# Layer 1 attention: each batch's second 128 queries taken in reversed blocks of 32, and one product of 512 columns for both halves

## The chip, the core and the metric

The kernel runs on one core of a Trainium2 chip. The metric is the time on the device in microseconds (us), as the median of several runs; less is better. The engines named below work side by side, each through its own instructions in order: PE (matrix products), DVE (vector work), ACT (scalar functions and copies), POOL (general work and gathers by index), SP (starts most transfers).

## The reference

Two transformer layers on x of 8 batches x 256 tokens x 128 channels. Each layer adds attention and a mixture of experts, both computed from the same normalised input. The change is in layer 1's attention:

```python
q = (x @ Wq + bq).reshape(B, T, 8, 128);  kv = x @ Wkv + bkv      # 8 query heads, one key and value head
q = q + pe;  k = k + pe                                           # the same table of positions
scores = einsum('bhqd,bkd->bhqk', q, k) / sqrt(128)
scores = where(tril(ones(T, T)), scores, lowest)                  # causal
out = softmax(scores) @ v                                         # then heads side by side
return out @ Wo
```

with T = 256 here. Layer 0's attention has 16 heads of 8 channels and no mask. Both layers' experts pick tokens by a router; layer 0 takes two experts of eight per token and a shared one, layer 1 takes one of eight.

## The kernel before

All of it is float32, and every matrix product runs as two passes over PE. The order of the work is written out by hand: a call wrapped in `seq` keeps its place in the program on its engine, and tables (`at_place`, `at1`, read by `between` and `fill`) name the steps that are put between the attention's own. Layer 0 goes through its 8 batches with the routing, the experts, the shared expert (`shared_up`, `shared_down`) and, at the end, the first three blocks of layer 1's norm between them. Layer 1 goes through its 8 batches with its own router and experts between them.

**Norm and projections.** `Norm.turned` transposes a block of 512 normalised tokens with PE into a tile of the PSUM pool `one` (tag `bank`, three buffers taken in turn; a fourth, `held`, is for one long-lived tile) and ACT copies it into `xT`, channels on partitions, 2048 tokens in order. `l1_values` makes values and router logits from it (line 784), `l1_project` queries for 8 heads and keys (line 807), to which DVE adds bias and positions (line 814). `l1_scale` multiplies the query weights, biases and positions (`peq_s`) by 1/sqrt(128) on POOL, once. POOL also builds the constants at the start (`more_constants`); the norm's reciprocal roots (lines 303 and 304) are POOL instructions behind them.

**Layer 1's attention.** A batch has three parts: `u[0]` is the first 128 queries of all 8 heads against 128 keys, `u[1]` and `u[2]` are the second 128 queries of 4 heads each against 256 keys. For each part:
- `l1_scores` (line 1281): PE, into a tile of 1024 columns of the PSUM pool `big`, which has two such tiles;
- `l1_maxima` (lines 1291 and 1295): DVE adds the causal mask to the 128 columns on the diagonal and takes the maximum;
- `l1_exp` (line 1301): ACT, one exponential and sum per head;
- `l1_weigh` (line 1313): the division by the sum, on POOL, or on DVE for the parts in `ON_VECTOR`;
- `l1_turn` (line 1328): DVE transposes 32x32 blocks into `pT`, one tile for each half, so that keys lie on partitions: the 32 queries of block n lie in rows 32n to 32n+31.

`l1_pv(b, t, po)` (line 1345) then multiplies with the values. Block n of the queries uses strip n of PE, rows 32n to 32n+31, and its own PSUM bank `po[n]`; the four strips work side by side. The values lie in `vrep`, a copy for each strip, written by `l1_spread`. Block n of half t needs key blocks 0 to 4t+n. Each product has 8 heads x 32 queries = 256 columns:

```python
for j in range(NQ1 * (t + 1)):
    for n in range(NQ1):
        end = NQ1 * t + n
        if j <= end:
            r = ROW * n
            ...
            rhs=pT[r : r + ROW, :, j, :],
```

`l1_out` (line 1358) copies the four banks into `oT` with ACT, and `l1_finish` (line 1364) multiplies by Wo and lets DVE add to `acc`. The products of batch b-1 stand in batch b (`l1_previous`), between the scores of `u[1]` and those of `u[2]`:

```python
l1_exp(u[0])
l1_previous(b)
...
l1_weigh(u[0])
l1_scores(u[2])
```

For the last batch they stand at the end of the program, the halves apart. Buffers in the pool `work` have two copies by default; `oT`, the second half's `pT`, layer 0's attention result and the shared expert's hidden values share tag `c`, the first half's `pT` and layer 0's queries `qa` share tag `h`.

## Time and profile before

| | us |
|---|---|
| median of 3 runs | 591.26 (590.09 to 594.53) |
| the profiled execution | 584.82 |
| its span, first to last instruction | 583.0 |
| busy in it: PE, its weight loads, DVE, ACT, POOL | 497.3, 354.1, 359.4, 246.6, 205.6 |
| line 1345, the products with the values | PE busy for 48.9, 576 records, two per product |
| mean granted TensorE clock | 0.938 |

The profile is of one execution. A line in a view reads: start and length, engine, source line, operation, the tiles it writes and reads (out<-in), shapes and count; in brackets, how long the engine stood idle before it and what ended the wait. A timeline line merges neighbours of one kind. "PEld" is PE's weight loads. In a table of waits the columns are the total, how often, and the longest, in us. The granted clock is 1.0 or 0.5, and a mean over a stretch lies between them. Layer 0 ends near 336 us; layer 1's eight batches begin their scores near 334, 358, 379, 412, 458, 497, 527 and 541 us.

### The profile page before, as it was taken

What the parts mean: (1) busy time and instruction counts of PE and PEld (TensorE: products, weight loads), DVE (VectorE), ACT (ScalarE), POOL (GpSimd) and SP (SyncE); (2) the same over time, 40 slices, a digit from 0 to 9 for tenths busy, and PEclk for the clock granted to TensorE, in tenths of its full rate; (3) what the DMA queues carried; (4) which work ended last, traced back from release to release, by engine and by line L of the source; (5) the groups of instructions that cost most, each with busy time, mean ns of one, the idle gap of its engine ahead of it and who ended that gap; (6) DMA issues with size and microseconds to landing.
All of it is one profiled execution on the core that took longest, in us unless ns stands there. A gap on an engine that the chain in (4) does not pass through costs nothing.

```text
span 583.0 us, 11267 instructions
## 1 busy us (share of the span) xinstructions
PE 497.3 (85%) x3996; PEld 354.1 (61%) x3996; DVE 359.4 (62%) x733; ACT 246.6 (42%) x681; POOL 205.6 (35%) x254
## 2 busy tenths in 40 slices
PE   4887688889998899967899968877969989989777
PEld 1633345656766577543554736666667878978666
DVE  5487954646756467637797467787633544527662
ACT  4616123434443254313443551523255584665161
POOL 6230023266432440274372032212576041124740
PEclk9999786989999799989999997996989999999977
DMA  3600411324443231011021130171048465512111
GB/s 108 189 1 19 133 33 44 110 72 121 126 128 105 74 77 38 28 46 29 17 69 45 37 92 19 37 200 41 25 108 234 145 149 180 158 55 64 33 32 56
DMA packets 61925, 47.78 MB, mean 82 GB/s; under 512 B 6389, under 2 KB 56781, under 8 KB 61869
## 3 DMA queue, kind: packets, MB, share of 16 engines
q1 hardware_dynamic: 57453, 38.59, 23.3%
q0 software_dynamic: 3840, 8.26, 5.9%
q8 instruction: 32, 0.52, 0.4%
q10 hardware_dynamic: 576, 0.20, 0.1%
q14 instruction: 24, 0.20, 0.1%
HBM read 38.78 MB, written 8.26 MB: 81 GB/s over the span
## 4 chain that ended last, share of the span: by engine, by line
PE 56%; DVE 20%; issue 9%; ACT 6%; POOL 4%; DMA 1%; SPq 0%; another core or an unknown queue 0%; POOLq 0%; ACTq 0%; DVEq 0%
PE s L894 7%; PE u L692 6%; PE pv L967 5%; PE s L1281 4%; PE d L709 4%; DVE mx L909 4%; PE u L1210 3%; PE o L1345 3%; PE d L1228 3%; PE qk L807 3%; PE s L940 3%; PE wo L1364 3%; ACT p L1301 2%; PE ds L760 2%; PE sh L745 2%
## 5 line engine op out<-in xcount | busy, mean ns | idle before, releaser
L952 ACT ACTIVATE eT<-s 128x1024 f32<-128x1024 f32 x64 | 65.5, 1024 | 138.9 <-PE s L940 95.7
L909 DVE TENSOR_REDUCE mx<-s 128x4 f32<-128x1024 f32 x64 | 77.7, 1220 | 32.0 <-PE s L940 14.3
L513 POOL DMA_INDIRECT xs<-xd,idx x62 | 63.0, 1016 | 67.0 <-issue 57.8
L894 PE MATMUL s<-qk 32*128 32x256 f32 x512 | 74.4, 422 | 13.6 <-DVE mx L909 8.8
L1313 POOL TENSOR_TENSOR p<-p,rec 128x1024 f32<-128x1024 f32 x21 | 39.8, 1896 | 112.3 <-DVE rec L1311 112.2
L1301 ACT ACTIVATE p<-s,m 128x256 f32<-128x256 f32 (+1 forms) x128 | 52.5, 443 | 62.5 <-DVE m L1295 51.0
L940 PE MATMUL s<-qa,qk 32*128 32x256 f32 x512 | 75.6, 414 | 2.5 <-DVE qa L921 2.3
L894 PEld LDWEIGHTS s<-qk 32*128 32x128 f32 x512 | 43.2, 195 | 41.7 <-DVE mx L909 17.9
L513 POOL DMA_INDIRECT yt<-yg,idx x48 | 48.9, 1020 | 47.1 <-issue 37.2
L1281 PE MATMUL s<-kT,qT 128*128 128x128 f32 (+1 forms) x256 | 49.8, 348 | 9.1 <-ACT p L1301 4.3
L940 PEld LDWEIGHTS s<-qa,qk 32*128 32x128 f32 x512 | 45.9, 192 | 10.6 <-DVE qa L921 5.0
L1345 PE MATMUL o<-pT,vrep 32*128 32x256 f32 x576 | 48.9, 407 | 3.9 <-DVE pT L1328 2.2
L1281 PEld LDWEIGHTS s<-kT,qT 128*128 128x128 f32 x256 | 40.0, 200 | 18.2 <-issue 6.9
L1345 PEld LDWEIGHTS o<-pT,vrep 32*128 32x128 f32 x576 | 40.5, 197 | 11.6 <-DVE pT L1328 2.4
L692 PE MATMUL u<-xg,gu_s 128*88 128x128 f32 x312 | 42.6, 278 | 1.6 <-issue 1.6
L967 PE MATMUL pv<-eT,va 128*32 128x256 f32 x512 | 39.3, 412 | 1.5 <-issue 1.4
L692 PEld LDWEIGHTS u<-xg,gu_s 128*88 128x88 f32 x312 | 37.1, 160 | 3.8 <-issue 3.8
L1219 ACT ACTIVATE h<-u,own_b 128x128 f32<-128x128 f32 x92 | 25.9, 375 | 27.7 <-PE u L1210 25.2
L1291 DVE TENSOR_TENSOR s<-s,mask 128x512 f32<-128x512 f32 (+1 forms) x24 | 20.9, 869 | 25.2 <-PE s L1281 21.5
L1364 PE MATMUL wo<-wo_s,oT 128*128 128x128 f32 x256 | 34.0, 297 | 2.1 <-DVE qT L814 1.8
L1364 PEld LDWEIGHTS wo<-wo_s,oT 128*128 128x128 f32 x256 | 33.0, 212 | 3.9 <-issue 3.3
L1328 DVE STREAM_TRANSPOSE pT<-p 128x1024 f32<-128x1024 f32 x24 | 29.5, 1232 | 7.1 <-POOL p L1313 7.1
(222 smaller groups left out, 843.2 us busy)
## 6 DMA issues: line engine op xcount, KB each, us to landing
w_up<-in_w_dram SPq DMA_DIRECT2D x30, 256.0 KB
gu_s<-in_gu_dram SPq DMA_DIRECT2D x39, 176.0 KB
vrep<-vd SPq DMA_DIRECT2D x32, 128.0 KB
w_down<-in_w_dram SPq DMA_DIRECT2D x16, 256.0 KB
yg<-ys SPq DMA_DIRECT2D x14, 256.0 KB
dn_s<-in_dn_dram SPq DMA_DIRECT2D x39, 88.0 KB
bias<-in_b_dram SPq DMA_DIRECT2D x23, 64.0 KB
acc<-in_x_dram SPq DMA_DIRECT2D x4, 256.0 KB
```

The lines of the kernel that those rows point to most:

```text
L513: seq(nc.gpsimd.indirect_dma_start(out=dst, out_offset=None, in_=table, in_offset=bass.IndirectOffsetOnAxis(ap=idx[:, k : k + 1], axis=0), ...
L692: seq(nc.tensor.matmul(ps[:IC, ts(c, P)], lhsT=gu0_s[:, i % RING0, c, :], rhs=xg0.get(i), start=True, stop=True,))
L894: seq(nc.tensor.matmul(pv[:, jj, t, :], lhsT=qT[r : r + ROW, g, ds(o + t * P, P)], rhs=kT[r : r + ROW, g, ds(o, S)], start=True, stop=True,))
L909: seq(nc.vector.tensor_reduce(m[:, ds(2 * half, 2), :, D0 * ((g + 1) % NG)], pv, AX.X, ALU.max, negate=True))
L940: seq(nc.tensor.matmul(pv[:, jj, c, :], lhsT=kT[r : r + ROW, g, ds(o + c * P, P)], rhs=qa[r : r + ROW, g, :], start=True, stop=True,))
L952: seq(nc.scalar.activation(eT.rearrange("p j c q -> p (j c q)"), ps, AF.Exp, scale=SC0))
L967: seq(nc.tensor.matmul(po[ds(ROW * j, ROW), ts(g % 2, S)], lhsT=va_flat[:, ds(o, ROW)], rhs=eTs[j // 2][:, j % 2, c, :], start=(c == 0), s ...
L1281: seq(nc.tensor.matmul(u.sc[:, h, :], lhsT=qT[:, u.h0 + h, ds(o + u.t * P, P)], rhs=kT[:, ds(o, u.nk)], start=True, stop=True,))
L1301: seq(nc.scalar.activation(u.p[:, h, :], u.sc[:, h, :], AF.Exp, bias=u.m[:, h : h + 1], accum_out=u.sums[:, h : h + 1],))
L1313: seq(engine.tensor_tensor(u.p, u.p, rec[:, : u.nh].unsqueeze(2).to_broadcast([P, u.nh, u.nk]), ALU.mult))
L1345: seq(nc.tensor.matmul(po[n][:, ts(t, H1 * ROW)], lhsT=vrep[r : r + ROW, b % 2, j, :], rhs=pT[r : r + ROW, :, j, :], start=(j == 0), stop= ...
L1364: seq(nc.tensor.matmul(ps[:, ts(t, P)], lhsT=oT[:, h, ts(t, P)], rhs=wo1_s[:, h, :], start=(h == 0), stop=(h == H1 - 1),))
```

## The change

The second 128 queries of each batch are laid out with their blocks of 32 in reverse order, so strip n holds block n of the first half and block 7-n of the second, with n+1 and 8-n key blocks. For that:
- `xT` holds 384 columns for a batch: its 256 tokens in order and its second 128 again with the blocks reversed. For layer 1 `Norm.turned` makes the latter with two more products per block of 512 tokens, with a permutation matrix `reverse`, in another buffer of `bank`, and one more ACT copy. `queries` picks the first 128 and the reversed 128 for the query projection.
- `peq_s` has its second half reversed; the second half's mask is another one (`masks[1]`); POOL builds it and `reverse`.
- `pT` is one tile for a batch, 384 columns per head, and the transposes write into it with that stride. It has one buffer, as have `oT`, the shared expert's hidden values and `ot0`; `qas` holds layer 0's two `qa` tiles by hand.
- `l1_pv` takes both halves in one call, except for the last batch. On strips 1 to 3 the key blocks 0 to n, which both halves need, are products of 512 columns; the rest have 256. The products of the four strips are issued in the order of the columns that stand before them on their strip.
- `l1_out` puts block 7-n back in its place.

Lines that are only moved to the new layout of `xT` are left out below.

```diff
@@ -231,7 +231,11 @@
     SC1 = 1.0 / math.sqrt(P)
     def l1_scale():
-        for dst, src in ((wq1_s, wq1_s), (bq1_s, bq1_s), (peq_s, pe_s)):
+        pairs = [(wq1_s, wq1_s), (bq1_s, bq1_s), (peq_s[:, :P], pe_s[:, :P])]
+        for n in range(P // ROW):
+            pairs.append((peq_s[:, ds(P + ROW * n, ROW)], pe_s[:, ds(S - ROW * (n + 1), ROW)]))
+        for dst, src in pairs:
             seq(nc.gpsimd.tensor_scalar_mul(dst, src, SC1))
     tri = ctile([P, P], "tri")
@@ -242,7 +246,8 @@
     lane_h = const.tile([P, P], F16, tag="lane_h", name="lane_h")
     token_h = const.tile([P, NTILE], F16, tag="token_h", name="token_h")
     token = ctile([P, NTILE], "token")
-    mask = ctile([P, P], "mask")
+    masks = [ctile([P, P], f"mask{t}") for t in range(2)]
+    reverse = ctile([P, P], "reverse")
@@ -267,7 +272,22 @@
             ))
         seq(nc.gpsimd.tensor_copy(lane_h, lane))
         seq(nc.gpsimd.tensor_copy(token_h, token))
-        make_causal_mask(nc, mask, mask_val=MASKED)
+        make_causal_mask(nc, masks[0], mask_val=MASKED)
+        seq(nc.gpsimd.memset(masks[1], 0.0))
+        for n in range(P // ROW):
+            rows = masks[1][ds(ROW * n, ROW), :]
+            seq(nc.gpsimd.affine_select(
+                out=rows,
+                in_=rows,
+                compare_op=ALU.is_ge,
+                fill=MASKED,
+                base=P - ROW * (n + 1),
+                pattern=[[-1, P]],
+                channel_multiplier=1,
+            ))
+            seq(nc.gpsimd.tensor_copy(
+                reverse[:, ds(ROW * n, ROW)], ident[:, ds(P - ROW * (n + 1), ROW)]
+            ))
     dram = ctx.enter_context(tc.tile_pool(name="dram", bufs=1, space=bass.MemoryType.DRAM))
@@ -284,7 +304,15 @@
         ))
-    xT = ctile([P, NT], "xT")
+    xT = ctile([P, B, 3 * P], "xT")
+    def tokens(n):
+        return xT[:, n // 2, ds(n % 2 * P, P)]
+    def block(blk):
+        return xT[:, ds(2 * blk, 2), :S]
     class Norm:
@@ -326,7 +354,21 @@
             ps = bank(f"lnT_{self.name}")
             for t in range(TPB):
                 seq(nc.tensor.transpose(ps[:, ts(t, P)], self.xn[:, t, :], ident))
-            seq(nc.scalar.copy(xT[:, ts(self.blk, BLK)], ps))
+            seq(nc.scalar.copy(block(self.blk), ps.rearrange("p (b s) -> p b s", b=2)))
+            if self.layer:
+                ps = bank(f"lnR_{self.name}")
+                for t in range(2):
+                    seq(nc.tensor.matmul(
+                        ps[:, ts(t, P)],
+                        lhsT=self.xn[:, 2 * t + 1, :],
+                        rhs=reverse,
+                        start=True,
+                        stop=True,
+                    ))
+                seq(nc.scalar.copy(
+                    xT[:, ds(2 * self.blk, 2), S:],
+                    ps[:, :S].rearrange("p (b s) -> p b s", b=2),
+                ))
     def softmax8(lg, nm, n):
...
@@ -739,13 +781,13 @@
     def shared_up(blk, c):
         n = CH[c]
         if c == 0:
-            hs0[blk] = work.tile([P, len(CH), BLK], F32, tag="c", name=f"hs_{blk}")
+            hs0[blk] = work.tile([P, len(CH), BLK], F32, tag="c", name=f"hs_{blk}", bufs=1)
         ps = [bank(f"sh_{blk}_{c}_{k}") for k in range(2)]
         for k in range(2):
             seq(nc.tensor.matmul(
                 ps[k][:n, :],
                 lhsT=shu_s[:, k, ds(P * c, n)],
-                rhs=xT[:, ts(blk, BLK)],
+                rhs=block(blk),
                 start=True,
                 stop=True,
             ))
...
@@ -796,6 +838,9 @@
     qk1 = {}
+    def queries(blk):
+        return xT[:, ds(2 * blk, 2), :].rearrange("p b (t c) -> p b t c", t=3)[:, :, 0:3:2, :]
     def l1_project(blk):
         qT = work.tile([P, H1, BLK], F32, tag="qk", name=f"qT1_{blk}")
@@ -807,7 +852,7 @@
             seq(nc.tensor.matmul(
                 ps,
                 lhsT=wk1_s if h < 0 else wq1_s[:, h, :],
-                rhs=xT[:, ts(blk, BLK)],
+                rhs=block(blk) if h < 0 else queries(blk),
                 start=True,
                 stop=True,
             ))
@@ -910,13 +955,15 @@
             m[:, ds(2 * half, 2), :, D0 * ((g + 1) % NG)], pv, AX.X, ALU.max, negate=True
         ))
+    qas = work.tile([P, 2, NG, S], F32, tag="h", name="qas", bufs=1)
     def l0_augment(b):
         qT, _ = qk[b // 2]
         ps = bank(f"mT_{b}")
         for t in range(2):
             seq(nc.tensor.transpose(ps[:, ts(t, P)], mx[b % 2][:, t, :], ident))
-        qa = work.tile([P, NG, S], F32, tag="h", name=f"qa_{b}")
+        qa = qas[:, b % 2]
         for g in range(NG):
             seq(nc.vector.scalar_tensor_tensor(
                 qa[:, g, :],
@@ -977,7 +1024,7 @@
     def l0_normalise(b, gp, po, at):
         nm = f"{b}_{gp}"
-        ot = work.tile([P, 2, NQ, ROW], F32, tag="c", name=f"ot0_{nm}")
+        ot = work.tile([P, 2, NQ, ROW], F32, tag="ot0", name=f"ot0_{nm}", bufs=1)
         seq(nc.vector.transpose(ot.rearrange("p g n r -> p (g n r)"), po))
         rec = small.tile([P, 2, NQ], F32, tag="rec0", name=f"rec0_{nm}")
         seq(nc.vector.reciprocal(rec, ot[:, :, :, D0]))
...
@@ -1289,7 +1338,7 @@
     def l1_maxima(u):
         diag = u.sc[:, :, ds(u.t * P, P)]
         seq(nc.vector.tensor_tensor(
-            diag, diag, mask.unsqueeze(1).to_broadcast([P, u.nh, P]), ALU.add
+            diag, diag, masks[u.t].unsqueeze(1).to_broadcast([P, u.nh, P]), ALU.add
         ))
         u.m = small.tile([P, H1], F32, tag="m1", name=f"m1_{u.name}")
         seq(nc.vector.tensor_reduce(u.m[:, : u.nh], u.sc, AX.X, ALU.max, negate=True))
@@ -1321,40 +1370,53 @@
     def l1_turn(u):
-        if u.h0 == 0:
-            turned[u.b, u.t] = work.tile(
-                [P, H1, u.nk], F32, tag="c" if u.t else "h", name=f"pT_{u.name}"
-            )
+        if u.t == 0:
+            turned[u.b] = work.tile([P, H1, 3 * P], F32, tag="c", name=f"pT_{u.name}", bufs=1)
         seq(nc.vector.transpose(
-            turned[u.b, u.t][:, ds(u.h0, u.nh), :].rearrange("p h k -> p (h k)"),
-            u.p.rearrange("p h k -> p (h k)"),
+            turned[u.b][:, ds(u.h0, u.nh), ds(u.t * P, u.nk)], u.p
         ))
     def l1_banks(b):
         return [bank(f"o_{b}_{n}") for n in range(NQ1 - 1)] + [held(f"o_{b}")]
-    def l1_pv(b, t, po):
-        pT = turned[b, t].rearrange("p h (j q) -> p h j q", q=ROW)
-        for j in range(NQ1 * (t + 1)):
-            for n in range(NQ1):
-                end = NQ1 * t + n
-                if j <= end:
-                    r = ROW * n
-                    seq(nc.tensor.matmul(
-                        po[n][:, ts(t, H1 * ROW)],
-                        lhsT=vrep[r : r + ROW, b % 2, j, :],
-                        rhs=pT[r : r + ROW, :, j, :],
-                        start=(j == 0),
-                        stop=(j == end),
-                    ))
+    def l1_pv(b, tt, po):
+        pT = turned[b]
+        calls = []
+        for n in range(NQ1):
+            last = (n, NK1 - 1 - n)
+            if len(tt) == 1 or n == 0:
+                order = [((t,), j) for t in tt for j in range(last[t] + 1)]
+            else:
+                order = [(tt, 0), *(((1,), j) for j in range(n + 1, last[1] + 1))]
+                order += [(tt, j) for j in range(1, n + 1)]
+            at = 0
+            for t, j in order:
+                end = order[-1] == (t, j) or (n == 0 and j == last[t[0]])
+                calls.append((at, n, t, j, j == 0, end))
+                at += len(t)
+        for at, n, t, j, start, stop in sorted(calls):
+            r = ROW * n
+            blocks = pT[r : r + ROW, :, ds((t[0] * NQ1 + j) * ROW, ROW)]
+            if len(t) > 1:
+                blocks = pT[r : r + ROW, :, : 2 * P].rearrange(
+                    "p h (t k) -> p t h k", t=2
+                )[:, :, :, ds(j * ROW, ROW)]
+            seq(nc.tensor.matmul(
+                po[n][:, ds(t[0] * H1 * ROW, len(t) * H1 * ROW)],
+                lhsT=vrep[r : r + ROW, b % 2, j, :],
+                rhs=blocks,
+                start=start,
+                stop=stop,
+            ))
     def l1_out(tt, po, oT):
         for n in range(NQ1):
             src = po[n].rearrange("p (t h q) -> p t h q", t=2, h=H1)
-            dst = oT.rearrange("p h (t q) -> p t h q", t=2)[:, :, :, ds(n * ROW, ROW)]
+            dst = oT.rearrange("p h (n q) -> p n h q", q=ROW)[:, n : NK1 - n : NK1 - 1 - 2 * n]
             seq(nc.scalar.copy(dst[:, tt], src[:, tt]))
     def l1_finish(b, tt, oT):
@@ -1448,11 +1510,10 @@
         nonlocal oT
         if b > 0:
             po = l1_banks(b - 1)
-            for t in range(2):
-                l1_pv(b - 1, t, po)
+            l1_pv(b - 1, (0, 1), po)
             if b + 1 < B:
                 l1_spread(b + 1)
-            oT = work.tile([P, H1, S], F32, tag="c", name=f"oT_{b - 1}")
+            oT = work.tile([P, H1, S], F32, tag="h", name=f"oT_{b - 1}", bufs=1)
             l1_out(slice(None), po, oT)
     for b in range(B):
@@ -1493,12 +1554,12 @@
             fill(b, 2)
     po = l1_banks(b)
-    l1_pv(b, 0, po)
-    oT = work.tile([P, H1, S], F32, tag="c", name=f"oT_{b}")
+    l1_pv(b, (0,), po)
+    oT = work.tile([P, H1, S], F32, tag="h", name=f"oT_{b}", bufs=1)
     l1_out(ds(0, 1), po, oT)
     l1_turn(u[2])
     fill(b, 2)
-    l1_pv(b, 1, po)
+    l1_pv(b, (1,), po)
     l1_out(ds(1, 1), po, oT)
     l1_finish(b, (0,), oT)
     fill(b, 3)
```

More of the change, by code (lines that the diff above doesn't have):

```diff
@@ L544, in l0_values @@
                 seq(nc.tensor.matmul(
-                    pv[:, t, :], lhsT=xT[:, ts(t2 + t, P)], rhs=wvg0_s, start=True, stop=True
+                    pv[:, t, :], lhsT=tokens(t2 + t), rhs=wvg0_s, start=True, stop=True
                 ))
@@ L561, in l0_project @@
         seq(nc.tensor.matmul(
-            ps, lhsT=(wq0_p, wk0_p)[n], rhs=xT[:, ts(blk, BLK)], start=True, stop=True
+            ps, lhsT=(wq0_p, wk0_p)[n], rhs=block(blk), start=True, stop=True
         ))
@@ L785, in l1_values @@
                     pv[:, t, :],
-                    lhsT=xT[:, ts(n + t, P)],
+                    lhsT=tokens(n + t),
                     rhs=wvg1_s,
@@ L1008, in keep_warm @@
             ps = bank("warm")
-            seq(nc.tensor.matmul(ps, lhsT=ident, rhs=xT[:, :BLK], start=True, stop=True))
+            seq(nc.tensor.matmul(ps, lhsT=ident, rhs=block(0), start=True, stop=True))
     def first_scores(i):
```

## The prediction

> **What bounds the kernel now.** I read the totals first, then the busy time by stretch, then the products that the change rebuilds (line 1345) and the waits after them. By stretch (columns: stretch, its length, busy PE, PE weight loads, DVE, ACT, POOL, granted clock, DMA):
>
> ```profile
> 285.00:336.00 51.00, 49.04 (x328) 27.98 (x328) 35.18 (x87) 22.63 (x43) 20.95 (x26) 1.00 0.16 47
> 350.00:379.00 29.00, 24.80 (x162) 18.68 (x163) 22.66 (x44) 9.99 (x42) 7.58 (x4) 0.88 0.10 28
> 458.00:497.00 39.00, 36.38 (x302) 32.06 (x301) 18.12 (x30) 24.12 (x78) 8.87 (x7) 1.00 0.61 170
> ```
>
> PE is close to full at the end of layer 0 (285 to 336, from 295 on with gaps under 0.2 us) and in the middle of layer 1; around 350 to 412 it waits more. The group itself and the wait behind it:
>
> ```profile
> L1345 PE MATMUL o<-pT,vrep 32*128 32x256 f32 x576 | 48.9, 407 | 3.9 <-DVE pT L1328 2.2
> ...
> PE 56%; DVE 20%; issue 9%; ACT 6%; POOL 4%; DMA 1%; SPq 0%; another core or an unknown queue 0%; POOLq 0%; ACTq 0%; DVEq 0%
> ```
>
> ```profile
> PEld s L1281 <- ACT p L1301: 5.6, 5, 2.8
> ```
>
> The first line looks like 49 us of PE work open to gain. The second view says what follows it: the next scores, l1_scores(u[2]) in line 1281, wait five times for ACT's exponentials, because they need a big PSUM tile that l1_exp(u[0]) must first have read (two such tiles). Batch 4 and batch 3 in the timeline:
>
> ```profile
> 461.37 5.46 PE L1345 MATMUL o<-pT,vrep 32*128 32x256 f32 x72
> ...
> 466.05 0.40 ACT L1301 ACTIVATE p<-s,m 128x128 f32<-128x128 f32 x1
> ...
> 466.76 1.59 PEld L1281 LDWEIGHTS s<-kT,qT 128*128 128x128 f32 x8 [0.33 <-ACT p L1301]
> ```
>
> ```profile
> 415.73 6.20 PE L1345 MATMUL o<-pT,vrep 32*128 32x256 f32 x72
> ...
> 419.44 0.40 ACT L1301 ACTIVATE p<-s,m 128x128 f32<-128x128 f32 x1
> ...
> 421.86 1.99 PE L1281 MATMUL s<-kT,qT 128*128 128x256 f32 x8
> ```
>
> End of the products / end of the exponentials / start of the scores, from the timeline: b=1 366.7/367.7/367.8; b=2 390.0/392.2/392.4; b=3 421.9/419.8/421.9; b=4 466.8/466.5/466.8; b=5 506.0/505.6/505.9; b=6 535.7/535.7/535.9; b=7 552.8/556.2/556.4. (Ends of matmuls include some drain.) Only in b=3 does PE hold the scores back by a real amount.
>
> **The products, part by part.** Strip n now makes n+1 products for the first half and n+5 for the second: 6, 8, 10, 12. A product is two passes; where one strip runs alone its passes start 216 ns apart, where four run each still starts every 216 ns. So the longest strip sets 12 x 2 x 0.216 = 5.18 us, and with the first load 5.46. Reversed, every strip has 9: 3.89, some 4.15 with the load: 1.30 less in each of seven batches (the last keeps its halves apart and has 4 + 8 steps as before). The 512-column sharing gives nothing beyond this: the projection's 512-column passes (line 807, four in 1.88 us) take 0.43 each, twice a 256-column one. It only lowers the count, 576 records to 450.
>
> Worth of the 1.30: nothing in b=1, 2, 4, 5, 6, 7, where the exponentials end last; PE's hole before the scores grows. In b=7 the first shared product also waits for the last transpose, where before the first half ran in its shadow:
>
> ```profile
> 545.08 2.01 PE L1345 MATMUL o<-pT,vrep 32*128 32x256 f32 x20
> 549.06 3.74 PE L1345 MATMUL o<-pT,vrep 32*128 32x256 f32 x52 [1.98 <-DVE pT L1328]
> 556.35 1.22 PE L1281 MATMUL s<-kT,qT 128*128 128x256 f32 x2 [3.55 <-issue]
> ```
>
> All nine steps then run after 549.1 and end near 553.1, with 3.2 us of cover until 556.35. In b=3 the scores can start at 420.0 instead of 421.9, if the 0.7 us by which these products exceeded 5.46 doesn't come back; 1.2 if it does. I take **-1.6**; behind it the maxima, the transposes and the first expert's gather matrix follow at once, and POOL's gathers for the second group end at 427.9, early enough.
>
> **The reversed tokens.** Each layer-1 norm block gets two more 128x128 matmuls (4 passes; by line 1210, eight passes in 1.06 us, 0.45 us) and one ACT copy (0.37, by the 128x256 copies of line 1358). More than their length counts that they take one more buffer of the three-bank PSUM pool, which turns in order, so each waits for the reader of the tile three allocations earlier. That the pool turns so is seen in these starts: L745 starts as L814 frees its bank, 310.23 + 0.7.
>
> ```profile
> 309.16 0.66 PE L328 MATMUL lnT<-ident,xn 128*128 128x128 f32 x4
> 309.72 1.12 PE L807 MATMUL qk<-xT,wq_s 128*128 128x512 f32 x2
> 311.03 1.99 PE L745 MATMUL sh<-xT,shu_s 128*128 128x512 f32 x4 [0.19 <-DVE qT L814]
> ```
>
> - Block 0 (near 290): the new product's bank is freed by DVE's line 677 at 292.0, where PE now runs pv (291.1 to 292.1). pv and line 745 come 1.4 late; DVE had 0.86 of slack before its next line 677, and the scores after it lose a wait they had. Net **+0.65**.
> - Block 1 (309): the projection moves one bank on and waits for line 814 until 311.0; line 745 starts at 312.0: **+1.0**, PE being full up to 336.
> - Block 2 (327): no bank is late; **+0.45**.
> - Block 3 (batch 0 of layer 1): here the values already wait for a bank,
>
> ```profile
> 345.10 1.36 PE L328 MATMUL lnT<-ident,xn 128*128 128x128 f32 x4
> 351.33 2.15 PE L784 MATMUL vg<-wvg_s,xT 128*128 128x136 f32 x8 [4.87 <-DVE kT L814]
> ```
>
> and the new product takes that place in the queue: it starts at 351.3, the values after it, at half clock (this stretch has it) 0.9 later, and DVE's router step, which waits for the values' logits (2.07 idle before 354.0), with them: **+0.85**. ACT's copies lie in its gaps.
>
> **The rest.** POOL's constants: a memset (0.2), four masks (by the causal mask, 0.28 each) and four copies (0.15 to 0.2 each) follow at 3.8, end near 5.6, and hold up the first norm step (line 303, at 5.30): **+0.3**, between 0 and 1. The four small scalings of the positions lie in batch 2 of layer 0 on an idle POOL. The strided form of the transposes (128x8x128, 128x4x256) isn't in the trace: same elements, so no less than 1.23 us; a row break costs at most the 0.03 us by which line 814 (two rows) exceeds line 678 (one), so 8 breaks 0.2, and 24 transposes 5 us, about half of them on the path. Nearest is line 814, so 0, upper end +2.5. Single buffers (pT, oT, hidden, ot0): each new writer stands behind its old readers on the same engine, or behind PE work that follows them, so nothing. If that were not so, a transpose would wait for the products, 4 us. At the end the copies of the last second half all wait for strip 0, now the longest: four of 0.37, starting 0.27 apart, end 1.2 after the products, under the 1.9 us of the first half's output product: nothing.
>
> **Two rules weighed.** The trace has clock 0.50 from 391.03 to 397.86 after a stretch (387.62 to 391.03) with PE busy for 2.35 of 3.41 us, so about 1 us of hole with only one strip active before it is enough there. The Trainium skill ("TensorE: Matmul & The Clock Gate", "Why this matters for your kernels") only asks for no idle gaps over some 3 us. By the page, the enlarged holes cost nothing new (only b=2 and b=7 exceed 3 us, and both are slow already); by the row, b=1 (hole 1.1, then 2.4) may get one slow window of 3.4 us, 1.7 us of PE time, half hidden. I take 0 and keep +1 to +2 for the range. Second, the same page ("Measured speedup vs the span model") gives four row strips 3.07x; the trace's 216 ns with one strip and with four is 4x. By the page nine balanced steps would last 3.89 x 4/3.07 = 5.1 us and even b=3 would gain only 0.1; I go by the trace.
>
> **Sum.** 0.65 + 1.0 + 0.45 + 0.85 + 0.3 - 1.6 = +1.65. The profiled execution took 584.82 (span 583.0), so 586.5; the median of the runs shown, 591.26, lies 6.4 above it, and I carry that over: **593.0**. A change of 1% (5.9 us) is what a measurement of this kernel can tell from none.
>
> **Rivals.**
> 1. Likeliest (0.60): small gains and losses as above, 589 to 597.
> 2. The saved PE time counts in every batch: 7 x 1.30 = 9.1 less, with the losses of 3.25: -5.9, so 585.4. For it: PE is 85% busy and holds 56% of the chain. Against: the list of ends above. 0.14, as the scores may be held by something that moves too.
> 3. On the slow side, the clock: the holes after the products, larger by 1.3 us, each bring a half-clock window of 3.4 us just where PE is full (b=4, 5, 6, and 1): 1.7 us each, 4 x 1.7 = 6.8 on top of 593.0: 599.8. It decides from three such windows. Against: a hole of 1.3 leaves 62% busy, and most such windows in the trace stay fast. 0.14.
> 4. The transposes' new form or PE's reads with more strides are slow: +3 to +10, 596 to 603. 0.08. Against: today's reads already jump every 32 elements at full rate.
> 5. It doesn't do what it says, the shared products serialise the strips: they would then last 7 us or more, past ACT's end, +1.5 in six batches: 602. 0.04.
>
> The range 586.5 to 601 takes 1, most of 3 and 4. Within 1%: case 1, half of 4 and a share of 2 and 3; 0.65. Faster 0.13, slower 0.22.
>
> **What would show it.** The products at some 4.15 us a batch with 450 records; scores (line 1281) still ending a wait for ACT's line 1301, idle larger by 1.3; line 745 near 312 after a bank wait; values near 352 one product later; transposes at 1.23; the scores of b=3 right behind the exponentials. A scores start that follows the products at once in several batches would refute the main step; so would a mean clock below 0.92.

## The result, and the profile after

| | before, us | after, us |
|---|---|---|
| median of 20 runs each (lowest to highest) | 587.94 (582.54 to 594.53) | 592.72 (585.01 to 597.27) |
| profiled execution; its span | 584.82; 583.0 | 588.64; 586.9 |
| mean granted TensorE clock | 0.938 | 0.939 |
| busy PE, PE weight loads, DVE, ACT, POOL | 497.3, 354.1, 359.4, 246.6, 205.6 | 489.2, 343.4, 358.3, 247.8, 209.0 |

The ratio is 1.0073 (95% interval 1.0046 to 1.0101): some 4.3 us longer, and within 1%. On another chip, with the kernel before in the same comparison, it was 1.0007 (0.9981 to 1.0033). The ratios leave out executions more than 1.5% above the fastest of their kernel; on the first experiments' chip, where the kernel before alone scatters from 580.6 to 597.1 us, that drops half of its executions (34 of 68), so the tables below set the ratio of the means of all executions beside it.

TensorE is busy for 8.1 us less and the kernel is no shorter. The scores in the kernel before (busy, mean ns of one, idle just before and what ended most of it), then the chain in the page of the changed kernel, and two groups:

```profile
L1281 PE MATMUL s<-kT,qT 128*128 128x128 f32 (+1 forms) x256 | 49.8, 348 | 9.1 <-ACT p L1301 4.3
```

```profile
PE 52%; DVE 23%; issue 8%; ACT 7%; another core or an unknown queue 3%; POOL 3%; DMA 2%; SPq 2%; ACTq 0%; POOLq 0%; DVEq 0%
...
L1330 PE MATMUL s<-kT,qT 128*128 128x128 f32 (+1 forms) x256 | 46.3, 332 | 13.0 <-ACT p L1350 11.7
...
L1407 PE MATMUL o<-pT,vrep 32*128 32x256 f32 (+1 forms) x450 | 37.7, 458 | 4.6 <-DVE pT L1375 3.7
```

PE's share of the chain fell from 56% to 52%. Line 1407 is the old 1345, line 1330 the old 1281, line 1350 the old 1301. The products fell from 48.9 to 37.7 us; the idle time of the scores behind ACT rose from 4.3 to 11.7. The waits of the weight loads in layer 1 (total, times, longest) say the same, and show a newcomer, the reversing product of the last norm block:

```profile
PEld s L1330 <- ACT p L1350: 14.4, 7, 4.1
...
PEld lnR L361 <- DVE kT L859: 5.0, 1, 5.0
```

Batch 4 and batch 3 in the timeline of the changed kernel (start, length):

```profile
470.84 4.15 PE L1407 MATMUL o<-pT,vrep 32*128 32x256 f32 x54
...
475.51 0.40 ACT L1350 ACTIVATE p<-s,m 128x128 f32<-128x128 f32 x1
...
476.06 1.99 PE L1330 MATMUL s<-kT,qT 128*128 128x256 f32 x8 [1.07 <-ACT p L1350]
```

```profile
422.81 4.15 PE L1407 MATMUL o<-pT,vrep 32*128 32x256 f32 x54
...
426.51 0.40 ACT L1350 ACTIVATE p<-s,m 128x128 f32<-128x128 f32 x1
...
427.05 1.99 PE L1330 MATMUL s<-kT,qT 128*128 128x256 f32 x8
```

In batch 4 the products end 1.07 us before the scores may start, which is when ACT's last exponential is read out. In batch 3, too, the scores now come right behind that exponential. From the end of the products to the third part's scores the idle time was 1.10, 2.42, 0, 0, 0, 0.17 us in batches 1 to 6 before; it is 2.41, 3.72, 0.09, 1.07, 1.06, 1.47 now: 1.3 us more in batches 1, 2 and 6, less in 3, 4 and 5, where the products had ended last before.

The other side of the account is the branch of the reversed tokens (`lnR`), at blocks 0, 1 and 3 of the changed kernel:

```profile
296.88 1.48 PE L356 MATMUL lnT<-ident,xn 128*128 128x128 f32 x4
299.23 0.71 PE L361 MATMUL lnR<-reverse,xn 128*128 128x128 f32 x4 [0.87 <-DVE sg L719]
...
318.25 0.61 PE L361 MATMUL lnR<-reverse,xn 128*128 128x128 f32 x4
318.98 1.12 PE L852 MATMUL qk<-xT,wq_s 128*128 128x512 f32 x2
319.94 1.88 PE L787 MATMUL sh<-xT,shu_s 128*128 128x512 f32 x4
...
360.49 1.22 PE L361 MATMUL lnR<-reverse,xn 128*128 128x128 f32 x4 [4.78 <-DVE kT L859]
361.50 2.02 PE L826 MATMUL vg<-wvg_s,xT 128*128 128x136 f32 x8
```

I followed by how much each TensorE step of the changed kernel starts later than its twin in the kernel before. This lag goes from 7.20 us ahead of the first `lnR` to 10.17 at the values of block 3: +1.39, +0.2, +0.45 and +0.92 at the four blocks. Batch 3 gives back 1.89 (7.08 at its first scores, 5.19 at its third part's). Batches 4 to 7 give back another 1.4 (9.29 to 7.91), which I had not expected. The rest of the differences goes with where the half-clock stretches fell: the lag rose by 6.5 in layer 0 behind the start (47.8 us of half clock against 34.1), fell by 3.1 between block 3 and batch 3 (7.7 against 19.2), rose by 4.1 between batches 3 and 4 (10.2 against 3.4), and fell by 4.1 at the end (none against 13.0).

The branch's cost can be read in other profiles too. From the first transposes of block 0 to the values of block 3 it is 61.65 us in before, before_xt, before_consts and before_layout, 61.68 in rev_proj and best1 (no branch), and 64.63 to 64.66 in before_lnr, after, after_again, after_table and after_late_table (all with the branch): **3.0 us**, on all three chips and in the 20 runs' profile. (The other three profiles have 5.4 to 6.8 us of half clock inside, these at most 2.7.) How the first two blocks share it differs: +1.39 and +0.2 in after and before_lnr, +0.76 and +0.87 in after_again, after_table and after_late_table, where the projection waits 0.60 us for its bank in block 1.

### The profile page after: what moved, and what is told of

The parts are those of the page before. It is cut to its first block, busy times and chain, and to the rows that moved or that the text cites. A ratio compares the mean times of both kernels' runs of the same rounds, so it can differ in the third digit from the quotient of the medians.

```text
span 586.9 us, 11064 instructions
## 1 busy us (share of the span) xinstructions
PE 489.2 (83%) x3886; PEld 343.4 (59%) x3886; DVE 358.3 (61%) x733; ACT 247.8 (42%) x685; POOL 209.0 (36%) x267
## 4 chain that ended last, share of the span: by engine, by line
PE 52%; DVE 23%; issue 8%; ACT 7%; another core or an unknown queue 3%; POOL 3%; DMA 2%; SPq 2%; ACTq 0%; POOLq 0%; DVEq 0%
PE s L939 7%; PE pv L1014 6%; PE u L734 6%; PE d L751 4%; ACT p L1350 4%; PE qk L852 3%; PE s L987 3%; DVE mx L954 3%; PE d L1275 3%; PE s L1330 3%; DVE pT L1375 3%; PE u L1257 3%; PE sh L787 3%; DVE m L1344 2%
## 5 line engine op out<-in xcount | busy, mean ns | idle before, releaser
L954 DVE TENSOR_REDUCE mx<-s 128x4 f32<-128x1024 f32 x64 | 77.7, 1220 | 34.1 <-PE s L987 13.8
L987 PE MATMUL s<-qas,qk 32*128 32x256 f32 x512 | 75.4, 409 | 5.2 <-DVE qas L968 3.4
L555 POOL DMA_INDIRECT yt<-yg,idx x48 | 49.8, 1037 | 48.9 <-issue 38.3
L1330 PE MATMUL s<-kT,qT 128*128 128x128 f32 (+1 forms) x256 | 46.3, 332 | 13.0 <-ACT p L1350 11.7
L987 PEld LDWEIGHTS s<-qas,qk 32*128 32x128 f32 x512 | 45.5, 188 | 13.5 <-issue 5.8
L1330 PEld LDWEIGHTS s<-kT,qT 128*128 128x128 f32 x256 | 37.9, 191 | 21.9 <-ACT p L1350 15.2
L1014 PE MATMUL pv<-eT,va 128*32 128x256 f32 x512 | 41.3, 420 | 2.8 <-issue 2.7
L1407 PE MATMUL o<-pT,vrep 32*128 32x256 f32 (+1 forms) x450 | 37.7, 458 | 4.6 <-DVE pT L1375 3.7
L1407 PEld LDWEIGHTS o<-pT,vrep 32*128 32x128 f32 x450 | 30.4, 193 | 10.7 <-DVE pT L1375 3.7
L852 PE MATMUL qk<-xT,wq_s 128*128 128x512 f32 x64 | 34.2, 645 | 1.0 <-DVE qT L859 0.7
L719 DVE SCALAR_TENSOR_TENSOR sg<-sg,u 88x256 f32<-88x256 f32 x39 | 16.2, 416 | 29.9 <-ACT sg L718 22.3
L1426 PEld LDWEIGHTS wo<-wo_s,oT 128*128 128x128 f32 x256 | 30.8, 201 | 5.9 <-issue 3.4
```

Source lines behind the costliest of these rows:

```text
L555: seq(nc.gpsimd.indirect_dma_start(out=dst, out_offset=None, in_=table, in_offset=bass.IndirectOffsetOnAxis(ap=idx[:, k : k + 1], axis=0), ...
L852: seq(nc.tensor.matmul(ps, lhsT=wk1_s if h < 0 else wq1_s[:, h, :], rhs=block(blk) if h < 0 else queries(blk), start=True, stop=True,))
L954: seq(nc.vector.tensor_reduce(m[:, ds(2 * half, 2), :, D0 * ((g + 1) % NG)], pv, AX.X, ALU.max, negate=True))
L987: seq(nc.tensor.matmul(pv[:, jj, c, :], lhsT=kT[r : r + ROW, g, ds(o + c * P, P)], rhs=qa[r : r + ROW, g, :], start=True, stop=True,))
L1014: seq(nc.tensor.matmul(po[ds(ROW * j, ROW), ts(g % 2, S)], lhsT=va_flat[:, ds(o, ROW)], rhs=eTs[j // 2][:, j % 2, c, :], start=(c == 0), s ...
L1330: seq(nc.tensor.matmul(u.sc[:, h, :], lhsT=qT[:, u.h0 + h, ds(o + u.t * P, P)], rhs=kT[:, ds(o, u.nk)], start=True, stop=True,))
```

## Experiments

All ratios are to the kernel before on the same chip, in executions of the same comparison.

**First chip: the branch, the layout, the projection, the sharing.** (Kernel before: median 589.47.)

| kernel | median, us | ratio (95%) | means of all |
|---|---|---|---|
| before_lnr | 590.55 | 1.0102 (1.0065 to 1.0139) | 1.0042 |
| before_layout | 591.04 | 1.0071 (1.0035 to 1.0106) | 1.0035 |
| rev_proj | 589.99 | 1.0034 (0.9998 to 1.0069) | 1.0017 |
| after_unshared | 589.70 | 1.0038 (1.0005 to 1.0070) | 1.0037 |

*before_lnr* adds the branch to the kernel before:

```diff
             seq(nc.scalar.copy(xT[:, ts(self.blk, BLK)], ps))
+            if self.layer:
+                ps = bank(f"lnR_{self.name}")
+                for t in range(2):
+                    seq(nc.tensor.matmul(ps[:, ts(t, P)], lhsT=self.xn[:, 2 * t + 1, :],
+                                         rhs=reverse, start=True, stop=True))
+                seq(nc.scalar.copy(xR[:, ds(2 * self.blk, 2), :], ...))
```

> The kernel before plus the reversed tokens alone: for each of the four blocks of layer 1's norm the two reversing products, their PSUM bank and the ScalarE copy, into a tile that nothing reads, with the four GpSimd copies that build the permutation. The second half's product is not reordered. My theory: the new cost of the change is this branch, because each block has to take one more of the three small PSUM banks in turn; the traces of before and after show +1.39, +0.3, +0.45 and +0.92 us at the four blocks, so this kernel is about 3 us (0.5%) slower than the kernel before. Rival (the branch is hidden, and the change's loss is the lengthened start or a throttled clock): within 1 us of the kernel before.

Slower, as the theory said and the rival did not. In its trace the lag behind the kernel before goes from 0.24 us at block 0's transposes to 3.23 at block 3's values: 3.0 us of path, as in the changed kernel. The ratio's 6 us are more than that, the means of all executions give 2.5.

*before_layout* is the kernel before with the tile of 384 columns and all the new constants.

> The kernel before plus what the change does ahead of layer 1 only: the token tile with 384 columns for each batch (the third 128 stay unwritten and unread), the second mask and the permutation built on GpSimd at the start. Layer 1 is as before. My theory: only the start costs something, +0.7 us by the first transposes of the two traces (+0.3 was forecast), so the time is 0.3 to 1 us longer; the 7 us by which the profile of after lags at the end of layer 0 are half-clock windows of that one execution. Rival (the strided token tile or the constants slow layer 0): 3 to 7 us slower, and the profile lags by as much at the first norm of layer 1.

The first transposes start at 8.31 us as expected (7.65 before), but the time is 0.71% longer, or 0.35% by all executions, not 0.05 to 0.15%: the rival's size by the ratio (4.2 us), below it by the means (2.0). Its profile lags by 1.9 us at the first norm of layer 1, not by the rival's 3 to 7. More half clock is not the cause: the mean granted clock over its 22 executions is 0.935, as over the 68 of the kernel before. Tile and constants were then taken apart on other chips (below).

*rev_proj* drops the branch from the changed kernel; the projection reads the reversed blocks itself:

```diff
-                rhs=block(blk) if h < 0 else queries(blk),
+  x2 = xT[:, ds(2 * blk, 2), ds(P, P)].rearrange("p b (n r) -> p b n r", r=ROW)
+  (po[:, :, 0, :], xT[:, ds(2 * blk, 2), :P]), (po[:, :, 1, :]..., x2[:, :, ::-1, :])   # two products
```

> The changed kernel without the reversed copy of the tokens: no permutation, no reversing products, no third bank, no second ScalarE copy. The query projection itself reads each batch's second 128 tokens in reversed blocks of 32, as one of two products of 256 columns in place of one of 512. The balanced strips, the second mask and the shared products stay. My theory: it loses the +3 us of the branch and keeps the gain at batch 3 (1.9 us), so it is about 1 us faster than the kernel before (0.0 to 2 us) and 3 us faster than the changed kernel. Rival (the loss lies elsewhere: layout, constants, clock): still 3 to 4 us slower than the kernel before.

It is not below the kernel before: the theory's sign was not confirmed here, and 0.34% with an interval from -0.02% to 0.69% does not decide; the changed kernel did not run beside it. But the branch's 3.0 us are gone from its trace (61.68 us from block 0 to block 3, above). In its profile batch 3's gain is there (the lag falls from 0.25 us at its first scores to -1.63 at its third part's), and half-clock stretches of 10.2 us behind it (3.4 in the kernel before) stand against it. The read itself is free: twelve products of 256 columns take what six of 512 take.

```profile
490.17 2.75 PE L843 MATMUL qk<-xT,wq_s 128*128 128x256 f32 x12
```

```profile
497.64 2.74 PE L852 MATMUL qk<-xT,wq_s 128*128 128x512 f32 x6
```

(The first line is the timeline of rev_proj, the second that of the changed kernel.)

*after_unshared* splits every product of 512 columns:

```diff
-            if len(tt) == 1 or n == 0:
-                order = [((t,), j) for t in tt for j in range(last[t] + 1)]
-            else:
-                ...
+            order = [((t,), j) for t in tt for j in range(last[t] + 1)]
```

> The changed kernel with each product of 512 columns over both halves split into two of 256 columns, each half a group of its own in its bank: 9 products of 256 columns in each strip instead of 450 records in all for 576 of equal columns. My theory: the strips' balance alone shortens the stage, so probability times values stays at about 4.15 to 4.3 us a batch (before 5.46) and the time is within 1 us of the changed kernel's, about 4 us above the kernel before. Rival (the shared products carry the gain, by fewer instructions and weight loads): the stage goes back to over 4.8 us a batch.

Its timeline in batch 4:

```profile
472.08 4.17 PE L1402 MATMUL o<-pT,vrep 32*128 32x256 f32 x72
477.29 1.99 PE L1330 MATMUL s<-kT,qT 128*128 128x256 f32 x8 [1.04 <-ACT p L1350]
```

4.17 us with 72 records against 4.15 with 54: the balance alone shortens the stage, and the rival is out. Its time, 0.38% above the kernel before (2.2 us), was expected at about 4 and can't be set beside the changed kernel's, which did not run here. But the sharing was not worth nothing, as the table of the clean stretch below shows.

**Second chip: tile, constants, and ACT's table load.** (Kernel before: median 546.83; this chip ran the kernel before some 43 us faster.)

| kernel | median, us | ratio (95%) | means of all |
|---|---|---|---|
| before_xt | 546.83 | 1.0006 (0.9972 to 1.0039) | 0.9999 |
| after_late | 545.86 | 0.9990 (0.9962 to 1.0018) | 0.9994 |
| before_table | 545.10 | 0.9948 (0.9923 to 0.9973) | 0.9955 |
| after_table | 544.42 | 0.9936 (0.9910 to 0.9961) | 0.9940 |

*before_xt* has only the tile:

```diff
-    xT = ctile([P, NT], "xT")
+    xT = ctile([P, B, 3 * P], "xT")
```

> The kernel before with the token tile of 384 columns for each batch and nothing else (no new constants at the start; the third 128 columns unused). The run with the constants as well was 4.2 us above the kernel before (interval +2.1 to +6.3), and its first transposes came at 8.31 us in place of 7.65. My theory: the tile's strides cost nothing, since products and copies of two runs of 256 columns take as long as one of 512, so this kernel is within 1.5 us of the kernel before, its first transposes are at 7.65 again, and the constants are what cost. Rival (the strided tile slows copies or products in layer 0): again about +4 us with the first transposes at 7.65.

No difference within some 2 us either way, and block 0 to block 3 takes 61.65 us as before, so no cost of the strided tile is seen. Its first transposes are at 7.32 us.

*after_late* builds the second mask and the permutation inside `l1_scale`:

```diff
-        seq(nc.gpsimd.memset(masks[1], 0.0))   # and the loop behind it, out of more_constants
         for dst, src in pairs:
             seq(nc.gpsimd.tensor_scalar_mul(dst, src, SC1))
+        seq(nc.gpsimd.memset(masks[1], 0.0))   # and the loop behind it
```

> The changed kernel with the second mask and the permutation built on GpSimd behind the scaling of layer 1's query weights (about 141 us) in place of at the start. My theory: GpSimd is free for the first norm's reciprocal root at about 5.3 us again, the first transposes go from 8.35 to about 7.6 us, and what the run with constants and layout lost comes back: 0.7 us in the path, and up to 3 us in the time if the later start also shifts layer 0; so 1 to 3 us faster than the changed kernel (1 to 3 us above the kernel before). Rival (the start is hidden): as the changed kernel, +4 us.

POOL's norm step (line 331) in the changed kernel, then in after_late:

```profile
6.03 0.21 POOL L288 COPY reverse<-ident 128x32 f32<-128x32 f32 x1
6.20 0.24 POOL L331 TENSOR_SCALAR rs<-mv 128x4 f32<-128x4 f32 x1
```

```profile
5.69 0.24 POOL L331 TENSOR_SCALAR rs<-mv 128x4 f32<-128x4 f32 x1 [1.83 <-DVE mv L329]
```

In the changed kernel the step stands directly behind the last constant; in after_late POOL waits 1.83 us for DVE. The first transposes go from 8.35 to 7.84 us. The time is level with the kernel before, a little better than expected; since the changed kernel is level on a chip of this speed too (below), the constants cannot be given much of that.

*before_table* and *after_table* add one line each, so that ACT loads the exponential's table while it idles:

```diff
+        if b in (4, 5, 6):
+            early = small.tile([P, 1], F32, tag="early", name=f"early_{b}", bufs=1)
+            seq(nc.scalar.activation(early, ones[:, 0:1], AF.Exp))
         ...                                   # l1_scores(u[0]) and l1_exp(u[0]) behind it
```

> The kernel before with one added one-element exponential on ScalarE ahead of the first scores of batches 4, 5 and 6, so that the load of the exponential table (1.28 us in the trace) falls where ScalarE idles and the exponentials of the first part start earlier. My theory: in batches 4 and 5 the third part's scores wait for nothing in the kernel before (TensorE ends the probability-times-values products just then), so earlier exponentials bring at most 0.2 us there; the time is within 1 us of the kernel before. Rival (the exponentials are the path in both kernels): 3 us faster.

> The changed kernel with the same added exponential in batches 4, 5 and 6. My theory: the 1.30 us that the products lost in each batch became idle time of TensorE ahead of the third part's scores (1.07, 1.06 and 1.47 us in these three batches), which wait for the first part's exponentials; with the table loaded earlier these holes close and the saved time appears: 3 to 3.5 us faster than the changed kernel, level with the kernel before plus 1 us, and the holes are under 0.3 us in the trace. Rival (TensorE's time counts wherever it is saved, or something else holds the third scores): as the changed kernel, +4 us above the kernel before.

The holes did close. In the changed kernel's batch 4 the table load stood right before the exponentials, behind an idle ACT:

```profile
471.81 1.28 ACT L1350 ACT_TABLE_LOAD   x1 [4.07 <-DVE m L1344]
```

In after_table's batch 4 (its timeline, first of PE: products and scores; then of ACT: the early table load and the last exponential):

```profile
425.64 4.15 PE L1407 MATMUL o<-pT,vrep 32*128 32x256 f32 x54
429.72 2.00 PE L1330 MATMUL s<-kT,qT 128*128 128x256 f32 x8
```

```profile
422.56 1.28 ACT L1523 ACT_TABLE_LOAD   x1
...
429.04 0.40 ACT L1350 ACTIVATE p<-s,m 128x128 f32<-128x128 f32 x1
```

They are 0, 0 and 0.19 us where they were 1.07, 1.06 and 1.47. But before_table is 0.52% faster (2.8 us), where I had said within 1 us: the rival's number. And after_table, 0.64% faster than the kernel before, is only 0.12% from before_table: their intervals overlap, so with the table loaded early the whole times do not tell the changed kernel from the kernel before. ACT was the later engine twice in these batches, at the third scores (which the earlier exponentials do not move in the kernel before) and at the expert's products behind them, which wait for ACT's activations (`h`). The clean stretch below has 1.7 of the 2.8 us; where the rest lies is not shown. Everything on ACT comes earlier, and the longest of those waits in batch 5 shrinks, in the kernel before and in before_table:

```profile
511.95 1.16 PE L1228 MATMUL d<-w_down,h 128*128 128x128 f32 x8 [1.39 <-ACT h L1219]
```

```profile
472.43 1.16 PE L1228 MATMUL d<-w_down,h 128*128 128x128 f32 x8 [0.78 <-ACT h L1219]
```

**A clean stretch.** From batch 4's product stage to batch 7's no profile has any half clock, so these times (start of one to start of the other) can be set side by side over all chips:

| kernel | stretch, us | idle before third scores, batches 4, 5, 6 |
|---|---|---|
| before, before_xt, before_lnr, before_consts, before_layout | 83.6 to 83.7 | 0, 0, 0.16 |
| after_unshared | 83.6 | 1.04, 1.05, 1.45 |
| after, after_late, after_again, rev_proj | 82.3 to 82.4 | 1.07, 1.06, 1.47 |
| before_table | 82.0 | 0, 0, 0 |
| after_table, best1, after_late_table | 79.2 to 79.3 | 0, 0, 0.2 |

The balanced strips alone (after_unshared) bring nothing here: 3 x 1.3 us of TensorE time became idle time. With the sharing the stretch is 1.3 us shorter with the same holes. With the table loaded earlier the kernel before gains 1.7 and the changed one 3.1, so that 2.8 us lie between the two: only then does most of the saved 3.9 appear. (Up to 1.3 of the 2.8 may be the sharing's; after_unshared with the early table did not run.) The sharing's 1.3 us come from two expert steps (0.45 in batch 4, 0.85 in batch 5), whose PSUM tile had another last reader. Batch 5's in the changed kernel and in after_unshared:

```profile
520.09 1.16 PE L1275 MATMUL d<-w_down,h 128*128 128x128 f32 x8 [0.70 <-DVE ys L1284]
```

```profile
522.63 1.16 PE L1275 MATMUL d<-w_down,h 128*128 128x128 f32 x8 [1.55 <-ACT h L1266]
```

In the first the wait is for the reader of the small tile taken two before, in the second for that of the one taken three before; so by these waits the pool does not always turn in order. Why the allocation fell differently with fewer products I did not find out.

**Third chip: the changed kernel again, the constants alone, and a better version.** (Kernel before: median 545.68.)

| kernel | median, us | ratio (95%) | means of all |
|---|---|---|---|
| after_again | 548.34 | 1.0007 (0.9981 to 1.0033) | 1.0026 |
| before_consts | 547.12 | 1.0031 (1.0000 to 1.0063) | 1.0025 |
| best1 | 538.86 | 0.9861 (0.9819 to 0.9903) | 0.9879 |
| after_late_table | 541.98 | 0.9937 (0.9912 to 0.9962) | 0.9929 |

*after_again* is the changed kernel, with no edit.

> The changed kernel as it is, on the chip of the three kernels beside it. On other chips it was 0.73% above the kernel before (interval 0.46% to 1.01%). My theory: the same again, 1.005 to 1.010. Rival (the loss belongs to the half-clock windows of one chip): within 0.3% of the kernel before, in which case the runs on different chips are not to be set beside each other.

The rival's case: on this chip the change makes no difference by the ratio (0.26% by all executions). Ratios from different chips are therefore not to be subtracted, which takes the ground from the reading of after_late as a gain.

*before_consts* is the kernel before with the new constants at the start:

```diff
-        make_causal_mask(nc, mask, mask_val=MASKED)
+        make_causal_mask(nc, masks[0], mask_val=MASKED)
+        seq(nc.gpsimd.memset(masks[1], 0.0))   # then four affine_select and four copies, as in the change
```

> The kernel before plus the second mask and the permutation built on GpSimd at the start, and nothing else; nothing reads the permutation or the second mask. Constants and strided tile together cost 0.71%, the strided tile alone 0.06%, and the changed kernel with its constants built later was level with the kernel before. My theory: the constants cost 0.7 us at the first transposes and 2 to 4 us in the time (0.3% to 0.7%), the rest through where layer 0's work then falls; first transposes at about 8.3 us. Rival (the start costs its 0.7 us only): within 0.25% of the kernel before.

+0.31%, at the lower edge of the theory and just over the rival's bound; an interval that begins at 0 does not part them. The first transposes are at 8.33 us. Against this kernel, which shares its chip and its late start, the changed one goes from 1.2 us ahead at block 0 to 1.8 us behind at the values of block 3 and ends level (spans 544.0 and 544.1): the branch's cost and the gains cancel.

*best1* is rev_proj with the second mask built late and the added exponential; *after_late_table* is after_late with the added exponential.

> A version meant to beat both: the balanced strips and shared products of the change; no reversed copy of the tokens (the query projection reads the second 128 tokens in reversed blocks of 32 itself); the second mask built late; and the added one-element exponential in batches 4, 5 and 6. My theory: 1.9 us gained at batch 3 and some 3 us in batches 4 to 6, and no branch cost: 4 to 6 us (0.7% to 1.0%) faster than the kernel before. Rival (the branch of reversed tokens costs nothing on this chip): no faster than the kernel beside it that keeps this branch.

> The changed kernel with its constants built late and with the added exponential in batches 4, 5 and 6; the branch of reversed tokens stays. Beside the version without that branch this gives the branch's cost again. My theory: 3 us (0.5%) slower than the version without the branch, 1 to 3 us faster than the kernel before. Rival (the branch is hidden): level with the version without it.

best1 beats the kernel before by 1.4% (1.2% by all executions), more than expected, and the changed kernel beside it by 1.5%. The two differ by the branch (against the split projection), and 0.76% lies between them (0.50% by all executions, 2.7 us), so the rival is out, and the branch costs about what its banks said. after_late_table is 0.6% faster than the kernel before, a little more than expected. best1 has only seven executions behind it.

## Why the prediction was right, and which terms were off

The prediction called the change within 1% by the likeliest case, and it was; the reason is in the main the one given: PE's saving becomes idle time, and the branch costs what batch 3 gives back and more. That its 593.0 us (592.9 by its own sum) lies so close to the measured 592.72 is luck: it carried over a baseline of 591.26, the median of three runs, where 20 gave 587.94, and the change came at +4.3 where it said +1.65.

- **Products.** 4.15 us a batch with 450 records: as worked out from 9 steps of two passes at 216 ns. By the Trainium skill's factor for row strips ("TensorE: Matmul & The Clock Gate", "Measured speedup vs the span model") it was an estimated 5.1; the trace's row was the right one. That the 512-column form shortens the stage by nothing holds (4.17 against 4.15).
- **Worth of the saving.** The step "nothing where the exponentials end last" holds: new idle time of 1.3 us in batches 1, 2 and 6, of 1.07 and 1.06 in 4 and 5, and no gain from the balance alone in the clean stretch. In batches 4 and 5 the prediction's own list has the products ending last, by 0.3 and 0.4 us, so they were not among those; the scores there do come 0.2 us sooner behind the batch's first ones. Batch 7 keeps its cover, though its products ran 3.2 of 5.75 us at half clock: they wait for the last transpose and the scores behind them still wait for ACT.

```profile
557.18 5.75 PE L1407 MATMUL o<-pT,vrep 32*128 32x512 f32 x52 [3.29 <-DVE pT L1375]
564.26 1.99 PE L1330 MATMUL s<-kT,qT 128*128 128x256 f32 x8 [1.34 <-ACT p L1350]
```

- **Batch 3.** -1.6 forecast, -1.89 in the trace. On the faster chips, where these products take 5.46 us in the kernel before too, it is -1.15: the 1.2 that the prediction gave for that case. What lengthened them to 6.2 in the first profile stays open.
- **Not in the sum: -1.3** in batches 4 and 5, from PSUM tiles that another engine had left. "The sharing gives nothing" was true of the stage and not of the stretch.
- **The branch.** 0.65, 1.0, 0.45 and 0.85 were forecast, 2.95 in sum; 3.0 came. In after_again, after_table and after_late_table the first two blocks are close to the forecast, 0.76 and 0.87. In the profile of the 20 runs block 0 has the full wait (1.39), and in block 1 line 787 follows the projection with no wait, as DVE had freed the bank 0.65 us earlier against PE than in the kernel before.
- **Start.** 0.3 forecast, 0.7 measured (first transposes at 8.35 and 7.65; over all profiles 8.31 to 8.43 with all the constants at the start, 7.30 to 7.84 without). I had added the masks and copies by their length and ended them at 5.6; the trace has them ending at 6.24, as mask and copy take turns 0.35 and 0.28 apart.
- **The sum** was +1.65. By the terms as measured it is 0.7 + 3.0 - 1.9 - 1.3 = +0.5, and with the faster chips' batch 3 +1.25. On the third chip the ratio says +0.4, the means +1.4. In the 20 runs the ratio says +4.3, and some 3.8 of that are in none of the steps. In the one profile there half clock ahead of layer 1's first norm block lasted 47.8 us, against 34.1 in the kernel before; half of the difference, 6.9, is about the 6.5 by which layer 0 lags. But that is one execution of each. The later start does not in general bring more half clock: before_layout has it and the same mean clock as the kernel before (0.935, on the first experiments' chip), and the changed kernel's 20 runs have 0.933 (the clocks of the kernel before beside them are not on record). What the 3.8 us are stays open.
- **The clock rival** (bigger holes bring half-clock stretches where PE is full) fell: no profile has any in the clean stretch, whatever its holes. This agrees with the page's rule ("Why this matters for your kernels", no gaps over some 3 us); these holes are 1.0 to 1.5.
- **Transposes** 1233 ns each (1232 before), and no transpose waits for the single buffers' readers: nothing, as costed.

## What to carry to other kernels

Before shortening a stage, list for every repetition when it ends and when the other releaser of the next step ends; only the excess counts, and moving that other releaser (here one table load of 1.28 us) can be worth more than the shortening and makes it count. A tile more from a small pool can cost a wait beside its own length (here 3.0 us for four blocks of 0.45); a layout that the consumer can read itself, as the projection here reads reversed blocks at full rate, costs none. When a change is worth less than the scatter, compare stretches of the trace that carry no half clock, and not ratios across chips. A forecast that meets the number is to be checked term by term, and for its baseline.

## What the runs showed of the hardware

- The kernel before took a median of 589.47 us on one chip and of 546.83 and 545.68 on two others. Its mean granted clock over all executions was 0.935, 0.957 and 0.959, so some 77, 47 and 45 us at half clock. Half of that difference is some 15 us of the 43; the rest I can't place.
- A matrix operand with a negative stride over blocks of 32 columns streams at full rate: 2.75 us against 2.74 for the same columns in order.
- The third scores' idle times in batches 4 to 6 repeat within 0.05 us over all profiles with the same code, on all chips; these have full clock there.
